# x Wx of 10 steps ahead of an LSTM's first step in place of 12, that of the other 54 spread over 22 steps in place of 21

## The chip, the cores and the metric

The kernel runs on one core of a Trainium2 chip. The metric is the device time of one execution in microseconds (us); the time before is the median of three runs, 312.17 us (311.90 to 312.34). The core's engines work side by side, each through its own queue of instructions in order: TensorE multiplies matrices (the profile calls it PE, and its weight loads PEld), VectorE (DVE) and ScalarE (ACT) work on elements, GpSimd is POOL, and SyncE (SP) issues most of the transfers.

## The reference

An LSTM over 64 steps (batch 32, 256 inputs, 256 hidden) is followed by three dense layers on all its outputs, whose weights are +1 or -1, and a residual:

```python
xW = jnp.einsum('ntd,dg->ntg', x, Wx) + b
def step(carry, xw_t):
    prev_h, prev_c = carry
    a = xw_t + prev_h @ Wh
    i, f, o = (jax.nn.sigmoid(a[:, s * Hd:(s + 1) * Hd]) for s in range(3))
    g = jnp.tanh(a[:, 3 * Hd:])
    next_c = f * prev_c + i * g
    next_h = o * jnp.tanh(next_c)
    return (next_h, next_c), next_h
h = jnp.concatenate([hs, -hs], axis=-1)
h = relu(s0 * (h @ sign(k0))) * 2      # 512 -> 1024
h = relu(s1 * (h @ sign(k1))) * 2      # 1024 -> 1024
out = x + s2 * (h @ sign(k2))          # 1024 -> 256
```

Here `sign` stands for +1 where the boolean weight is true and -1 elsewhere (the loop over the gates is written out in the original). The data are 32-bit floats.

## The kernel before

The 64 steps are a chain: step t needs h of step t - 1. Beside that chain TensorE has two kinds of work which are spread over the steps as cover: x Wx of later steps, then the dense layers (FFN) on blocks of 16 finished steps.

**Layout.** The 256 hidden units are cut into four quarters, the batch of 32 sits beside each, so that 4 x 32 = 128 partitions are full. The gate products (`gates_from_h`, L304 to L315) of one step are 16 matmuls, each with a 128x32 weight load (h transposed) and Wh streaming past: for each of the two PSUM banks (three gates of 64 columns in one, the output gate in the other), two halves of the contraction and four quarters. x Wx (`x_part`, L245 to L256) has the same form with 256 columns; four such matmuls for one half k of one step are two units of work, a step is four units, 8 matmuls, and two steps share a PSUM bank (`x_bank`), which `evict_x` adds the bias to and stores as tile `xg` (L265). When a unit is left over, the four matmuls are made in two halves of 128 columns, a unit each (L283 to L286).

**One step** (`cell_step`, L322 to L345): sigmoid of two gates, tanh, sigmoid of the output gate on ScalarE (L325 to L327), kept, new and c on VectorE (L329 to L333), tanh on ScalarE (L335), h and its transpose on VectorE (L337, L342), and then the copies of x Wx of the next step into the gate banks by ScalarE (L319, L320), onto which the next gate products add.

**FFN.** `ffn_block` (L588) works on 16 steps: h is split into two parts of reduced precision (`split_h`, L361 and L362), layer 0 (L594), layer 1 (L620) and layer 2 (L607) are matmuls with 128x128 weight loads and 512 columns, one unit each, 192 units a block. `evict` (L365 to L370) takes each result out of PSUM with ScalarE and VectorE (L368, L369). Three blocks lie in the loop, 576 units. The fourth, `last_block` (L433 on), comes after the last step, and uses sums of weight quarters (`make_sum`, L418) that VectorE makes during the loop. The output of a block is turned, scaled and stored a part per step (`output`, L373; L392, L395, L387).

**The order of the work** is written by hand; each engine's queue has the order of the program. Ahead of the first step stand the loads (x and Wx first, then Wh: two loads on SyncE's queue and two on ScalarE's, L142 to L144), products that warm TensorE up (L646), x Wx of the first 8 steps, then that of steps 8 up to `AHEAD` (L683), and the copy of step 0 into the gate banks (L685). The loop over t (L705) issues in each step the gate products, the cell, a part of an output if one is waiting (L711), and as many units of work as the goal asks for (L717 to L720). For t below `X_STEPS` the work is x Wx, with the whole number

```python
goal = (t + 1) * total_x // X_STEPS if t < X_STEPS else (t + 1 - X_STEPS) * total_ffn // (T - X_STEPS)
```

and from `X_STEPS` on it is the FFN. Before, that is 208 units on 21 steps (two steps of nine units, at t = 0 and t = 10, and 19 of ten) and 576 on 43 steps (13 or 14 each).

Behind these in each step come the smaller jobs: the transposes of later x on VectorE, each with a request for another half block of x on SyncE's queue (`next_x`, L267; L232, L96), splits of h, and "chores": conversions of the boolean weights (w0 on ScalarE and VectorE, L208 and L209; w1 and w2 on ScalarE, L214 and L218). `load[0]` counts the larger VectorE jobs of the step, and some of the smaller ones wait for a step in which it is below 2. Chores start at t = 2, those of w2 at t = 24, the sums at t = 28.

Of the kernel before, what the change touches and what calls it, by code (L numbers as in the profile page):

```python
# [43 lines left out]
def lstm_ffn(ctx: ExitStack, tc: tile.TileContext, x, cond, wx_d, wh_d, b_d, k0_d, k1_d, k2_d, s0_d, s1_d, s2_d, out):  # L44
# [14 lines left out]

    GATES = (3, 0, 1, 2)  # L60

    AHEAD = 12
    X_STEPS = 21

    FIRST_CHORE = 2
    W2_STEP = 24
# [200 lines left out]
    def next_x(half):  # L267

        if half < 2 * NB:
            load[0] += 1  # L270
            turn_x(*divmod(half, 2))
            if half + 4 < 2 * NB:
                load_x(*divmod(half + 4, 2), [nc.sync])

    def x_products(t0, t1):

        for t in range(t0, t1, 2):
            p = x_bank(t)
            for s in range(2):
                for k in range(2):  # L280
                    start = s == 0 and k == 0
                    passes = min(left_over[0], 2)
                    if passes == 1:  # L283
                        x_part(p, t + s, k, slice(0, 2), start)
                        yield 1
                        x_part(p, t + s, k, slice(2, 4), False)  # L286
                    else:
                        x_part(p, t + s, k, slice(0, 4), start)
                    if s == 1 and k == 1:
                        evict_x(p, t)  # L290
                        half, left = divmod(t + 2, SB // 2)
                        if left == 2 and half + 1 < 2 * NB:
                            turns.append(half + 1)
                        if left == 6 and turns:
                            next_x(turns.popleft())
                    yield passes
# [50 lines left out]
    def split_h(i):  # L347

        b, s = divmod(i, SB // SH)
        if s == 0:  # L350
            hparts[b] = (
                hpool.tile([P, 2, TB], F32R, tag="hhi", name=f"hhi{b}"),
                hpool.tile([P, 2, TB], F32R, tag="hlo", name=f"hlo{b}"),
            )
        hi, lo = (p[:, :, ts(s, SH * N)] for p in hparts[b])
        full = hist.pop(i)
        if b == NB - 1:

            hi, lo = (a.rearrange("p k (n t) -> p k t n", n=N) for a in (hi, lo))
            full = full.rearrange("p k (t n) -> p k t n", n=N)  # L360
        nc.scalar.copy(hi, full)  # L361
        nc.vector.tensor_tensor(lo, full, hi, ALU.subtract)  # L362
# [319 lines left out]
    nc.vector.transpose(hT, h_first.rearrange("p (j b) -> p b j", b=2))  # L682
    for _ in x_products(SB // 2, AHEAD):  # L683
        pass
# [3 lines left out]
    def ffn():  # L688
        for b in range(NB - 1):
            yield from ffn_block(b)  # L690
        yield from last_block(NB - 1)
# [8 lines left out]

    work = x_products(AHEAD, T)
    total_x = (T - AHEAD) * 4
    total_ffn = (NB - 1) * (4 * FC0 + 2 * FC0 * FC1 + 4 * FC1)
    done = 0
    for t in range(T):  # L705
# [5 lines left out]
        if outputs:  # L711
            load[0] += 1
            if next(outputs[0], "end") == "end":
                outputs.popleft()
        if t == X_STEPS:
            work, done = ffn(), 0
        goal = (t + 1) * total_x // X_STEPS if t < X_STEPS else (t + 1 - X_STEPS) * total_ffn // (T - X_STEPS)  # L717
        while done < goal:
            left_over[0] = goal - done
            done += next(work)  # L720
        if t == X_STEPS - 1:
            next(work, None)

        if turns and load[0] < 2:
            next_x(turns.popleft())
        if splits and (load[0] < 2 or t >= X_STEPS or t == SH * splits[0] + 2 * SH - 1):
            split_h(splits.popleft())
        else:
# [4 lines left out]
            elif t >= W2_STEP and chores2:  # L733
                chores2.popleft()()
            if w0_parts and (load[0] < 2 or t == X_STEPS - 1):
                w0_parts.popleft()()
# [34 lines left out]
```

## Time and profile before

| | before |
|---|---|
| median of three runs | 312.17 us (311.90 to 312.34) |
| the profiled execution's own time | 312.77 us |
| its span | 311.0 us |
| TensorE matmuls busy | 304.9 us (98%) |
| VectorE busy | 177.6 us (57%) |
| ScalarE busy | 143.1 us (46%) |
| TensorE's granted clock | 1.00 throughout |
| start of the first gate products on the chain | 17.64 us |
| start of the FFN work on the chain | 81.91 us |
| start of the last gate products on the chain | 260.08 us |

Busy times are shares of the span, and the starts are counted from the span's beginning. "The chain" is the work that ended last, followed back step by step to what released it; one line of it gives the start, the length, the engine, the tile and the line, and how many instructions are merged in it. A line of the waits gives who waited for whom, the time in total, how often, and the longest. "issue" means that the engine waited for nothing that the profile shows. A line of landings gives the time from a transfer's issue to its end.

### The profile page before, as it was taken

The numbers are of one execution on the slowest core, as the hardware profiler recorded it, in microseconds if no ns is written. First come the engines' busy times: TensorE is split into PE (matmuls) and PEld (weight loads), VectorE is DVE, ScalarE is ACT, GpSimd is POOL, SyncE is SP. The second block draws the span as 40 slices with busy tenths as digits, with TensorE's granted clock in tenths as the row PEclk, the third lists the DMA queues.
The fourth block names the chain that finished last, engine by engine and source line by source line (L and its number), as shares of the span: only waits on it lengthen the run. The fifth ranks groups of instructions, "written<-read, shape, count | busy, mean of one in ns | idle before, by whom it ended". The sixth has DMA issues, their size and how long they took to land.

```text
span 311.0 us, 9795 instructions
## 1 busy us (share of the span) xinstructions
PE 304.9 (98%) x4138; PEld 242.4 (78%) x4138; DVE 177.6 (57%) x527; ACT 143.1 (46%) x512; POOL 6.6 (2%) x24
## 2 busy tenths in 40 slices
PE   7999999999999999999999999999999999999994
PEld 3888888787777777777777777777777777899994
DVE  2466767777673444455755444568564444599441
ACT  0224657774564543444633433356443333786320
POOL 5300000000000000000000000000000000000000
PEclk9999999999999999999999999999999999999999
DMA  6864001143000000000010000000410000031001
GB/s 186 210 185 108 6 10 49 36 93 67 3 2 0 2 2 0 3 2 0 2 38 14 22 1 2 2 2 6 98 34 2 3 0 2 25 80 32 2 0 68
DMA packets 27450, 10.88 MB, mean 35 GB/s; under 512 B 23560, under 2 KB 26632, under 8 KB 27408
## 3 DMA queue, kind: packets, MB, share of 16 engines
q1 hardware_dynamic: 24768, 8.66, 11.3%
q10 hardware_dynamic: 2400, 1.57, 1.8%
q8 instruction: 32, 0.52, 0.7%
q14 instruction: 10, 0.08, 0.1%
q0 software_dynamic: 240, 0.04, 0.1%
HBM read 8.16 MB, written 2.10 MB: 33 GB/s over the span
## 4 chain that ended last, share of the span: by engine, by line
PE 96%; DMA 1%; DVE 1%; SPq 0%; ACT 0%; issue 0%; ACTq 0%
PE p L620 30%; PE gates L308 20%; PE px L249 18%; PE p L594 8%; PE po L607 7%; PE gates L459 4%; PE r L459 2%; PE x L459 2%; PE po L564 2%; PE p L486 2%; DMA wx<-in_L_cond_Wx_dram 1%; SPq L96 0%; DVE a_7l L369 0%; DVE o L574 0%; PE p_bias L661 0%
## 5 line engine op out<-in xcount | busy, mean ns | idle before, releaser
L308 PEld LDWEIGHTS gates<-wh,hist 128*32 128x32 f32 x2016 | 54.6, 109 | 22.3 <-issue 13.4
L308 PE MATMUL gates<-wh,hist 128*32 128x192 f32 x2016 | 68.1, 275 | 0.0
L249 PE MATMUL px<-wx,xT 128*32 128x256 f32 (+1 forms) x1168 | 60.7, 355 | 0.4 <-DMA wx<-in_L_cond_Wx_dram 0.4
L325 ACT ACTIVATE sig<-gates 128x128 f32<-128x128 f32 x64 | 17.7, 277 | 79.8 <-PE gates L308 79.6
L249 PEld LDWEIGHTS px<-wx,xT 128*32 128x32 f32 x1168 | 42.2, 111 | 12.3 <-DVE xT L232 1.3
L329 DVE TENSOR_TENSOR kept<-sig,c 128x64 f32<-128x64 f32 x63 | 14.2, 225 | 49.1 <-ACT sig L325 48.8
L335 ACT ACTIVATE th<-c 128x64 f32<-128x64 f32 x64 | 16.4, 257 | 31.4 <-DVE c L333 31.4
L337 DVE TENSOR_TENSOR h<-sig,th 128x64 f32<-128x64 f32 x64 | 14.4, 225 | 20.7 <-ACT th L335 20.7
L265 DVE TENSOR_TENSOR xg<-px,bias 128x512 f32<-128x512 f32 x32 | 21.2, 670 | 2.8 <-PE px L249 2.3
L319 ACT COPY gates<-xg 128x192 f32<-128x192 f32 x64 | 20.0, 313 | 1.5 <-DVE xg L265 1.5
L594 PE MATMUL p<-hhi,w 128*128 128x512 f32 x48 | 19.3, 402 | 0.0
L594 PE MATMUL p<-hlo,w 128*128 128x512 f32 x48 | 19.1, 397 | 0.0
L342 DVE STREAM_TRANSPOSE hist<-h 128x64 f32<-128x64 f32 x64 | 15.7, 245 | 2.4
L333 DVE TENSOR_TENSOR c<-kept,new 128x64 f32<-128x64 f32 x64 | 14.4, 225 | 2.2
L327 ACT ACTIVATE sig<-gates 128x64 f32<-128x64 f32 x64 | 14.9, 233 | 0.1
L326 ACT ACTIVATE cand<-gates 128x64 f32<-128x64 f32 x64 | 14.0, 218 | 0.0
L331 DVE TENSOR_TENSOR new<-sig,cand 128x64 f32<-128x64 f32 x64 | 13.9, 217 | 0.0
L320 ACT COPY gates<-xg 128x64 f32<-128x64 f32 x64 | 13.0, 203 | 0.0
L594 PEld LDWEIGHTS p<-hhi,w 128*128 128x128 f32 x48 | 9.0, 188 | 2.1
L594 PEld LDWEIGHTS p<-hlo,w 128*128 128x128 f32 x48 | 9.0, 188 | 1.9
L214 ACT ACTIVATE w<-bits,nsgn,sgn 128x1024 fp32r<-128x1024 uint8 x8 | 9.9, 1240 | 0.0
L620 PE MATMUL p<-a_7h,w 128*128 128x512 f32 x24 | 9.9, 412 | 0.0
(250 smaller groups left out, 603.1 us busy)
## 6 DMA issues: line engine op xcount, KB each, us to landing
x<-in_x_dram SPq DMA_DIRECT2D x52, 64.0 KB, 2.7
out_dram<-o SPq DMA_DIRECT2D x28, 64.0 KB, 1.8
bits<-in_L_ffn_k_dram SPq DMA_DIRECT2D x10, 128.0 KB, 2.7
wx<-in_L_cond_Wx_dram SPq DMA_DIRECT2D x2, 256.0 KB, 4.8
wx<-in_L_cond_Wx_dram ACTq DMA_DIRECT2D x4, 128.0 KB, 5.1
wh<-in_L_cond_Wh_dram ACTq DMA_DIRECT2D x2, 256.0 KB, 5.3
wh<-in_L_cond_Wh_dram SPq DMA_DIRECT2D x2, 256.0 KB, 5.8
k<-in_L_ffn_k_dram SPq DMA_DIRECT2D x2, 256.0 KB, 3.1
```

The lines of the kernel that those rows point to most:

```text
L249: nc.tensor.matmul(p[q * N : (q + 1) * N, t % 2, slots], xT[i // 2, i % 2][:, s, k, :], wx_q[:, k, q, slots], start=start, stop=False, ski ...
L265: nc.vector.tensor_tensor(xg[t], p.rearrange("p t g j -> p t (g j)"), b, ALU.add)
L308: nc.tensor.matmul(g[q * N : (q + 1) * N], hT[:, k, :], wh_q[:, k, q, slots], start=False, stop=(k == 1), skip_group_check=True,)
L319: nc.scalar.copy(gates[0], x_t[:, :3])
L325: nc.scalar.activation(sig[:, 0:2, :], gates[0][:, 1:3], AF.Sigmoid)
L327: nc.scalar.activation(sig[:, 2, :], gates[1][:, 0], AF.Sigmoid)
L335: nc.scalar.activation(th, c, AF.Tanh)
L342: nc.vector.transpose(hT, h.rearrange("p (j b) -> p b j", b=2))
L459: nc.tensor.matmul(bank[pair][:, i], a(k)[:, ts(2 * pair + i, P)], b(k, n), start=first and i == 0 and k == 0 and n == 0, stop=last and k ...
L594: nc.tensor.matmul(p, w0[:, k, ts(m, P)], a[:, k, :], start=(n == 0), stop=(n == 3))
L607: nc.tensor.matmul(po[m], w2[:, m, k], a1[k][n], start=(k == 0 and n == 0), stop=(k == FC1 - 1 and n == 1))
L620: nc.tensor.matmul(p1[m], w1[:, k, ts(m, P)], a0[k][n], start=(k == 0 and n == 0), stop=(k == FC0 - 1 and n == 1),)
```

## The change

Two constants. `AHEAD` says how many steps' x Wx is made ahead of the first step, `X_STEPS` over how many steps that of the rest is spread, and with it at which step the FFN begins.

```diff
     GATES = (3, 0, 1, 2)
 
-    AHEAD = 12
-    X_STEPS = 21
+    AHEAD = 10
+    X_STEPS = 22
```

What follows from the formula of the goal: x Wx of steps 10 and 11 moves from ahead of the loop into it; the loop's x Wx is (64 - 10) x 4 = 216 units on 22 steps, nine units at t = 0, 5, 11 and 16 and ten elsewhere; the FFN's 576 units lie on 42 steps, 30 of 14 units and 12 of 13. The smaller jobs come in partly other steps, since they follow the goal and `load[0]`: the four VectorE halves of the w0 conversions at t = 2, 10, 12 and 18 (before 6, 10, 14 and 18), the transposes of later x at t = 0, 3, 6, 9, 14 and 16 (before 0, 2, 5, 9, 13 and 15), the output of the first two blocks one step later, and the last sum of weight quarters at t = 60 (before 58). Each engine has the same instructions, in another order on TensorE, VectorE, ScalarE and SyncE.

## The prediction

> **What bounds the kernel now.** I read the page's busy shares first, then the chain of work that ended last (its shares, then its pieces in order of time), then the waits, and last the landings of the transfers that the first step needs.
>
> ```profile
> span 311.0 us, 9795 instructions
> PE 304.9 (98%) x4138; PEld 242.4 (78%) x4138; DVE 177.6 (57%) x527; ACT 143.1 (46%) x512; POOL 6.6 (2%) x24
> ...
> PE 96%; DMA 1%; DVE 1%; SPq 0%; ACT 0%; issue 0%; ACTq 0%
> ```
>
> TensorE is busy for 98% of the span and is 96% of the chain, so the time is a sum of TensorE work plus what little it waits. The chain in order of time (start, length, what) shows each step of the recurrence as a pair, its gate products (L308) and the cover behind them (L249 while x Wx lasts, L594, L620 and L607 afterwards):
>
> ```profile
> 10.74 6.91 PE px L249 x128
> 17.64 0.86 PE gates L308 x30
> 18.50 1.96 PE px L249 x40
> 20.46 0.92 PE gates L308 x32
> 21.38 2.16 PE px L249 x48
> 23.55 0.87 PE gates L308 x32
> ...
> 48.71 1.95 PE px L249 x40
> 50.66 0.93 PE gates L308 x32
> 51.59 2.16 PE px L249 x40
> ...
> 81.03 0.87 PE gates L308 x32
> 81.91 3.17 PE p L594 x13
> 85.08 1.01 PE gates L308 x32
> ...
> 103.03 3.40 PE p L620 x14
> 106.43 1.01 PE gates L308 x32
> ```
>
> The reader is to see three step lengths. With ten units of x Wx a step is 3.034 us (21.38 to 48.71 holds nine of them and 51.59 to 81.91 ten: 27.33 and 30.32 us). With nine units, at t = 0 and t = 10, it is 2.88 us (18.50 to 21.38, 48.71 to 51.59). In the FFN part a step of 13 units is 4.18 us (81.91 to 86.09) and one of 14 is 4.41 us (103.03 to 107.44); every FFN step from 81.91 to 260.08 has one of these two lengths, so nothing but TensorE's own work sets it.
>
> From the waits, one line (time in total, how often):
>
> ```profile
> PEld gates L308 <- issue: 13.4, 38, 0.4
> ```
>
> A weight load of the gates sat idle 0.35 us, with no releaser, in most of the 42 steps whose gates follow FFN work. Last, the answer for wh's two loads on ScalarE's queue (issued at 7.39 and 8.71 us), used below:
>
> ```profile
> DMA to landing us min/median/max: 3.8/5.3/6.7
> ```
>
> **The change, part by part.** The sum is made on this profiled execution, whose span is 311.0 us and whose own time is 312.77; the median of the three timed runs is 312.17, so the sum's difference is put on 312.17. A run differs from another by up to 0.44 us (311.90 to 312.34).
>
> 1. Ahead of the first step, x Wx of steps 10 and 11 goes: 2 steps x 8 matmuls = 16 matmuls of 128x256. The piece 10.74 to 17.64 holds 64 of them in 6.91 us (its x128 counts a load and a matmul each), 0.108 us apiece: -1.73 us. With them one addition of the bias (L265, 0.67 us) moves behind step 0; VectorE has room there, since it waits for TensorE in that stretch.
>
> 2. The x part of the loop has 54 x 4 = 216 units on 22 steps in place of 208 on 21. By the goal's whole numbers that is 18 steps of ten and 4 of nine (t = 0, 5, 11, 16), where before there were 19 and 2. 18 x 3.034 + 4 x 2.88 = 66.13 us against 19 x 3.034 + 2 x 2.88 = 63.41: +2.73 us. Split matmuls (two of 128 columns for one of 256) cost nothing: steps listed x48 and x40 both take 2.16. A nine-unit step should be one unit, 0.216, shorter than 3.034, that is 2.818; it measures 2.88, so its cover is too short by 0.06 us, and the chain sigmoid, cell, tanh, transpose shows through. Two more such steps are 0.13 of the 2.73.
>
> 3. The FFN part has 576 units on 42 steps in place of 43: 30 steps of 14 and 12 of 13, where before there were 17 and 26. 13 x 4.405 - 14 x 4.18 = -1.26 us. Why it is not zero: 14 units less 13 are 0.225 us, so a step has 4.18 - 13 x 0.225 = 1.25 us that are no FFN unit, while among x products the gates cost 0.87. The passage from FFN products (128x128 weights) to the gates (128x32 weights) and back costs 0.38 us a step: gates longer by 0.14, and 0.24 that the step's 13 units take beyond their pace. One passage of 43 goes.
>
> 4. What the earlier start uncovers. The first gate product (t = 0) would be issued 1.73 us earlier: its first matmul starts at 17.42 in the timeline, so at 15.69. It needs hT_first (transposed by 15.07), the copies of x Wx into its bank (by 12.84), and wh. The last wh load (slot 0, ScalarE's queue) was issued at 8.71 and landed 6.7 us later, at 15.41. A landing releases its reader some 0.16 to 0.22 us later (wx on SyncE's queue: 1.65 + 4.3 = 5.95, first product 6.11; x: 1.20 + 4.0 = 5.20, transpose 5.42). So wh is usable at 15.57 to 15.63: 0.06 us before it is wanted. Behind the waiting gate stand x products of TensorE's queue and all later steps, so any lateness is paid in full. Lower bound: nothing (no earlier start can gain more than 1.73). Upper bound: the four wh loads took 3.8, 5.0, 6.5 and 6.7 us, so a landing may be later by as much as the middle ones differ from the last, 6.7 - 5.3 = 1.4. I take +0.1, near the row of this very load.
>
> The Trainium skill (DMA: Bandwidth & Descriptors, Latency and other measured facts) speaks against the change here: it puts HBM access at 0.2 us on average and 2 us at high load, and this stretch moves some 180 GB/s. By the page alone, a load that met the high figure would be 1.8 us later (an estimate, 2 less 0.2) and take the whole earlier start back; this load's own row has it just in time.
>
> 5. Work that is only shifted against the steps. VectorE per x step keeps at most two large pieces behind the cell's own five: two of L265 (0.67), L232 (0.70), L209 (0.73) or one and L362 (0.47). In the three new short steps they are 22's addition with a split of h (t = 5), 36's with a split (t = 11), 48's with a transpose of x and a w1 conversion on ScalarE (t = 16). The two old short steps carried L265 with L232 (t = 0) and L265 with L209 and a w1 conversion of 1.24 us on ScalarE (t = 10): both fitted, kept (L329) starting 0.30 us after sig as everywhere. So the new ones are costed at nothing; without that cover each piece of 0.70 us too many would be paid once. In FFN steps VectorE's heaviest load (t = 51: a transposition, three L369, one L362) is the same as before, and TensorE there is ahead of a chain of 1.9 us by cover of 3.17 or more. SyncE's queue issues the same 43 rows; x of steps 48 to 63 is requested at t = 0 and t = 3 in place of t = 0 and t = 2, wanted many steps later. The four transfers for x of steps 16 to 23 land by about 16.4 us and are wanted near 19, where they were wanted at 20.9. POOL's queue is untouched. The output of blocks 0 and 1 starts one step later (t = 37 in place of 36, t = 51 in place of 50), and the last sum of weight quarters goes from t = 58 to t = 60; its product comes at about 290 us. The last recurrence step has 14 units in both, so the tail, with its 0.54 us wait for a_7l, stays.
>
> Sum: -1.73 + 2.73 - 1.26 + 0.1 = -0.16 us. On 312.17 that is 312.0.
>
> **The rivals.** A difference under 0.2%, 0.62 us, can't be told from no change.
> - The likeliest: as summed, 312.0, within 0.2%.
> - No passage is saved: what item 3 counts for one is paid again elsewhere in the FFN steps. For: the 0.35 us idle has no releaser. Against: steps of 13 and of 14 differ by a pure unit. Then -1.73 + 2.73 - 0.87 (the moved gates at the cheap price in both places) + 0.1 = +0.2: 312.4, also within 0.2%.
> - Slower, wh late: the first gates wait for the last piece of wh. For: 0.06 us of room. Against: the room is not negative in this execution, and earlier loads in the same queue set the first x product too, so a late queue moves both. Each us beyond 15.6 costs a us; it decides from a wait of 0.9 (-0.26 + 0.9 = +0.64). With a wait of 1.2: 313.1.
> - Slower, short steps don't fit: VectorE's pieces delay kept in the three new places by half of an 0.7 us piece each: -0.16 + 3 x 0.35 = +0.9, 313.1. Against: the old short steps carried as much.
> - Faster, the waits at the end of the recurrence go too: shifted evictions free a_7l earlier, and 0.54 us fall away: -0.16 - 0.54 = -0.7, 311.5. Against: the last step's units and their order are unchanged.
>
> **How the numbers follow.** Chances: the sum 0.62, no saved passage 0.12, wh late 0.09, short steps 0.07, the tail 0.10. Same is the first two, 0.74; slower 0.09 + 0.07 = 0.16; faster 0.10. The predicted time is the likeliest case's, 312.0. With the runs' own 0.44 us of spread the first two cases reach from 311.6 to 312.6; the range goes to 311.4, which takes in the tail's case, and to 312.9, which leaves out the larger part of the two slow ones.
>
> **What would show it.** Right: the piece of x products ahead of the first gates is 5.18 us long, and the first gates start near 15.9 on the chain; 22 steps of x products, four of them 2.88 us long; FFN steps only of 4.18 and 4.41, thirty of the longer; start of the FFN part at 82.9 (81.91 - 1.73 + 2.73) and the last gates near 259.8 before any wait for wh. Wrong: a gap on TensorE ahead of the first gates released by the wh transfer (wh late); short steps above 2.95 (they don't fit); FFN steps of other lengths (no saved passage); no wait for a_7l near 263 (the tail). The prediction fails if any one stall of over 0.6 us appears that the trace of before hides, and the first gates are where the room is least.

## The result, and the profile after

The changed kernel takes 313.83 us (median of 6 runs, 313.64 to 315.76) against 312.12 us for the kernel before in the same comparison: a ratio of 1.0059, with a 95% interval from 1.0044 to 1.0073. It is slower by 1.7 us, where a difference inside 0.6 us was forecast. The profiled execution took 313.79 us, with a span of 312.0. The two profiled executions differ by only 1.0 us, since the one of before took 312.77, 0.6 above its median. By the starts on their chains the difference of the spans is -1.93 up to the first gates, +2.72 from there to the FFN's start, +0.48 from there to the last gates and -0.27 behind them.

```profile
span 312.0 us, 9797 instructions
PE 305.7 (98%) x4138; PEld 241.9 (78%) x4138; DVE 178.5 (57%) x527; ACT 143.4 (46%) x512; POOL 6.6 (2%) x24
...
PE 94%; DVE 2%; DMA 1%; ACT 1%; issue 0%; SPq 0%; ACTq 0%
```

The page's busy shares (its first part) hardly move. The shares of the chain of work that ended last (its fourth part) do: TensorE goes from 96% to 94%, ScalarE and VectorE together from 1% to 3%. Where they come in is seen in the chain in order of time (start, length, what), read at the start of the steps, at the end of x Wx and around the end of a block of the FFN:

```profile
10.53 5.18 PE px L249 x96
15.71 0.86 PE gates L308 x30
16.57 1.96 PE px L249 x40
18.53 0.92 PE gates L308 x32
19.45 2.16 PE px L249 x48
...
82.70 3.17 PE p L594 x13
85.87 1.01 PE gates L308 x32
86.88 3.40 PE p L594 x14
90.27 1.01 PE gates L308 x32
...
134.67 3.40 PE p L620 x14
138.07 0.83 PE gates L308 x16
138.98 0.29 ACT sig L325
139.29 0.23 DVE kept L329
139.52 0.15 DVE new L331
139.69 0.23 DVE c L333
139.94 0.26 ACT th L335
140.20 0.22 ACT gates L319
140.56 0.54 ACT a_7h L368
141.12 0.70 DVE a_7l L369
141.87 1.43 PE po L607 x5
143.29 1.01 PE gates L308 x32
```

The first lines answer to those shown of before: 5.18 us of x products in place of 6.91, short steps of 2.88 us (16.57 to 19.45), FFN steps of 4.18 (82.70 to 86.88) and 4.40. The lines from 138.98 to 141.87, on ScalarE and VectorE and then the products that waited for them, are new at this place. The step that begins with the gates at 138.07 (t = 35) lasts 5.22 us until the next gates, where one of 14 units lasts 4.41. The same stands at 199.68 (t = 49), with 5.24 us; before, such a wait stood only at t = 63. The waits name it (who waited for whom, in total, times, longest):

```profile
PEld po L607 <- DVE a_7l L369: 1.6, 3, 0.5
PEld po L607 <- ACT a_7h L368: 0.9, 2, 0.4
```

Before there was one such wait, the 0.54 us at t = 63:

```profile
PEld po L607 <- DVE a_7l L369: 0.5, 1, 0.5
```

It is the loop's last step, and it loses some 0.4 us (4.83 us from its gates to the last block's first products, where 14 units take 4.41).

The timeline of the changed kernel around 140 us (start, length, engine, line, and in brackets the idle time ahead and what ended it) shows how it comes about. a_7h and a_7l are the two parts that layer 1's last tile is split into when it is taken out of PSUM:

```profile
139.34 0.40 PE L620 MATMUL p<-a_7l,w 128*128 128x512 f32 x1
...
140.36 0.20 ACT L320 COPY gates<-xg 128x64 f32<-128x64 f32 x1
...
140.50 0.59 ACT L368 ACTIVATE a_7h<-p 128x512 fp32r<-128x512 f32 x1
...
140.72 0.39 PE L607 MATMUL po<-a_5l,w 128*128 128x512 f32 x1
...
141.12 0.69 DVE L369 SCALAR_TENSOR_TENSOR a_7l<-p,a_7h 128x512 fp32r<-128x512 f32 x1 [0.38 <-ACT a_7h L368]
...
141.14 0.49 PE L607 MATMUL po<-a_7h,w 128*128 128x512 f32 x1
```

Layer 1's last tile is complete when the matmul of 139.34 ends, at 139.74. Its eviction by ScalarE (a_7h, L368) starts at 140.50, right behind the cell's copies into the gate banks (L319, L320), because the program puts it behind them in ScalarE's queue. TensorE has six layer 2 products that don't need this tile, the last of them at 140.72, and then waits for a_7h and again for a_7l.

Why at every block now: 576 units on 42 steps are 13.714 a step, and a block of 192 units is exactly 14 steps. So each of the three blocks ends with a step; its last step begins 14 units before the block's end. The last 12 of these are layer 2 products, which the program puts behind layer 1's last tile, so that tile is completed by the step's second unit, early in the step, while ScalarE is still bound to the cell. With 43 steps a block was 14.33 steps, and only the third ended with one (the last step had 14 units in both kernels).

The sum over the FFN steps: from the FFN's start to the last gates the changed kernel takes 261.35 - 82.70 = 178.65 us against 260.08 - 81.91 = 178.17. The prediction had 1.26 less, 176.91. The difference of 1.74 us is (5.22 - 4.405) + (5.24 - 4.405) = 1.65 (4.405 us is the usual step of 14 units), and a rest of 0.09, of which some hundredths stand at the steps behind these two (4.19 and 4.23 us in place of 4.18). With the 1.65 the prediction's sum of -0.16 us becomes +1.5; measured are +1.7, and +1.5 lies inside the interval.

### The profile page after: what moved, and what is told of

Same layout as the page of the kernel before. It is cut to its first block, busy times and chain, and to the rows that moved or that the text cites. A ratio compares the mean times of both kernels' runs of the same rounds, so it can differ in the third digit from the quotient of the medians.

```text
span 312.0 us, 9797 instructions
## 1 busy us (share of the span) xinstructions
PE 305.7 (98%) x4138; PEld 241.9 (78%) x4138; DVE 178.5 (57%) x527; ACT 143.4 (46%) x512; POOL 6.6 (2%) x24
## 4 chain that ended last, share of the span: by engine, by line
PE 94%; DVE 2%; DMA 1%; ACT 1%; issue 0%; SPq 0%; ACTq 0%
PE p L620 29%; PE gates L308 20%; PE px L249 18%; PE p L594 8%; PE po L607 6%; PE gates L459 4%; PE r L459 2%; PE x L459 2%; PE po L564 2%; PE p L486 2%; DMA wx<-in_L_cond_Wx_dram 1%; DVE a_7l L369 1%; ACT a_7h L368 0%; ACT sig L325 0%; SPq L96 0%
## 5 line engine op out<-in xcount | busy, mean ns | idle before, releaser
L319 ACT COPY gates<-xg 128x192 f32<-128x192 f32 x64 | 20.0, 313 | 1.3 <-DVE xg L265 1.3
L320 ACT COPY gates<-xg 128x64 f32<-128x64 f32 x64 | 13.0, 203 | 0.0
L620 PE MATMUL p<-a_0h,w 128*128 128x512 f32 x24 | 9.7, 404 | 0.0
```

The costliest lines, as they stand in the source:

```text
L319: nc.scalar.copy(gates[0], x_t[:, :3])
L620: nc.tensor.matmul(p1[m], w1[:, k, ts(m, P)], a0[k][n], start=(k == 0 and n == 0), stop=(k == FC0 - 1 and n == 1),)
```

## The experiments

All were compared with runs of the kernel before on the same chip (medians of 312.19 to 312.27 us). Each variant has a name, by which later texts and the table speak of it.

**Two units earlier (e1_plus2).** The goals of the FFN are two units higher in the changed kernel.

```diff
-(t + 1 - X_STEPS) * total_ffn // (T - X_STEPS)
+min(total_ffn, (t + 1 - X_STEPS) * total_ffn // (T - X_STEPS) + 2)
```

> The changed kernel, with every FFN goal two units higher (the last step has 12 units in place of 14), so that the last two products of layer 1's last tile of a block fall into the step before the one that ends the block. Theory A (in the changed kernel 576 units on 42 steps make a block exactly 14 steps; layer 1's last tile is finished as the second unit of the block's last step, its eviction stands on ScalarE behind that step's cell, and layer 2 has only 6 units to cover it; two new waits of 0.8 us and the old one at t = 63): the waits for a_7h and a_7l are gone, 2 x 0.82 and some 0.4 at t = 63 come back: 313.83 - 2.0 = 311.8, or by the prediction's sum 312.12 - 0.26 - 0.4 = 311.5. Theory B (the cost lies in the earlier first step or in the 22 steps of x Wx): 313.8, since these are not touched.

Measured: 312.39 us, a ratio to before of 1.0004 (95% interval 0.9995 to 1.0013, as in the brackets of the later results). The loss is gone but for 0.2 us, and no wait for a_7h or a_7l by layer 2 is left. The chain at the same end of a block:

```profile
135.24 3.40 PE p L620 x14
138.63 1.01 PE gates L308 x32
139.64 2.94 PE po L607 x12
142.59 0.45 PE p L594 x2
143.04 1.01 PE gates L308 x32
```

The step is 4.41 us again. The cause in the FFN is shown: nothing about the x part was touched. But 312.39 is 0.6 above the expected 311.8, and 0.9 above what the prediction's sum would give, so something else costs. One part stands in the trace: the first 32 products of the last block (L486) take 7.48 us here and 7.26 in the changed kernel, since they wait for the last split of h (`hlo`, L362), which now comes after a shorter last step. This 0.22 us is in all three executions with the goals two units higher (42.01 us from the first of these products to the start of VectorE's last instruction) and in none of the others (41.78 to 41.80).

**The same alignment made in the kernel before (e2_aligned).**

```diff
         goal = (t + 1) * total_x // X_STEPS if t < X_STEPS else (t + 1 - X_STEPS) * total_ffn // (T - X_STEPS)
+        goal = {33: 178, 34: 192, 47: 370, 48: 384}.get(t, goal)
```

> The kernel before, with four of its 43 FFN goals moved: t = 33 at 178 units, 34 at 192, 47 at 370, 48 at 384, so that blocks 0 and 1 end with a step and layer 1's last tile is finished as that step's second unit; 12 and 21 stay. Theory A: two waits of 0.8 us appear: 312.12 + 1.6 = 313.8. Theory B: 312.1, as before.

Measured: 314.84 us, 1.0078 (1.0064 to 1.0092), 2.6 us slower than before. The two waits appear, in the same total as in the changed kernel (1.6 and 0.9 us with the third at t = 63), and the two steps take 5.24 and 5.22 us. The expectation was too low, because the edit does more: it puts four units in the step after the second block, which takes 2.82 us where 1.25 + 4 x 0.225 = 2.15 would do if the cell's chain were covered, another 0.67. 0.83 + 0.81 + 0.67 = 2.3 of the 2.6 us.

**Each constant alone.** X_STEPS at 22 with 12 steps ahead (e3_12_22), and 10 steps ahead with X_STEPS at 21 (e4_10_21):

```diff
-    X_STEPS = 21
+    X_STEPS = 22
```

> X_STEPS 22 alone, 12 steps ahead: 208 units on 22 steps, 10 of ten and 12 of nine, 42 FFN steps. Theory A: x part 10 x 3.034 + 12 x 2.88 - 63.41 = +1.49, FFN steps -1.26, two waits +1.64: 312.12 + 1.9 = 314.0. Theory B (earlier first step): no earlier start here, +1.49 - 1.26 = +0.2: 312.3.

Measured: 314.05 us, 1.0055 (1.0043 to 1.0068): 1.8 us slower, with steps of 5.22 us at t = 35 and t = 49. The alignment comes with X_STEPS alone.

```diff
-    AHEAD = 12
+    AHEAD = 10
```

> AHEAD 10 alone, 21 steps: 216 units, 15 steps of ten and 6 of eleven (3.25 us), FFN on 43 steps as before. Theory A: -1.73 + (15 x 3.034 + 6 x 3.25 - 63.41 = +1.60) = -0.13: 312.0. Theory B: the loss of the earlier start shows here too, 313.5 or more.

Measured: 312.86 us, 1.0017 (1.0008 to 1.0027). No wait at the ends of the first two blocks, but 0.6 us slower than before where the sum had 0.1 faster. So there is a cost beside the alignment. The profiled executions place a part of it ahead of the first gates (times in us by the timeline; x Wx's end is that of its last matmul ahead of the gates; e5_plus1 and e6_order are the changed kernel with edits to the FFN alone, described below):

| | steps ahead | start of x Wx | its end | first gates | gates less end |
|---|---|---|---|---|---|
| before | 12 | 6.11 | 17.65 | 17.42 | -0.23 |
| e2_aligned | 12 | 5.85 | 17.09 | 16.85 | -0.24 |
| e3_12_22 | 12 | 6.15 | 17.33 | 17.09 | -0.24 |
| changed | 10 | 6.05 | 15.71 | 15.48 | -0.23 |
| e4_10_21 | 10 | 5.61 | 15.45 | 15.49 | +0.04 |
| e1_plus2 | 10 | 5.73 | 15.23 | 15.51 | +0.28 |
| e5_plus1 | 10 | 5.62 | 15.33 | 15.61 | +0.28 |
| e6_order | 10 | 5.70 | 15.77 | 15.54 | -0.23 |

With 12 steps ahead the gates follow x Wx at once (matmuls overlap by 0.23 us). With 10 ahead the gates never start before 15.48 in these five executions, however early x Wx is done: counted from the usual overlap, they are late by 0.27 us in e4_10_21 and by 0.51 in e1_plus2 and e5_plus1, and not at all in the changed kernel and e6_order, where x Wx itself ended late enough. In e1_plus2's timeline:

```profile
9.81 5.42 PE L249 MATMUL px<-wx,xT 128*32 128x256 f32 x96
...
15.48 0.95 PEld L308 LDWEIGHTS gates<-wh,hT_first 128*32 128x32 f32 x32 [0.73 <-issue]
15.51 1.08 PE L308 MATMUL gates<-wh,hT_first 128*32 128x192 f32 x32 [0.28 <-issue]
```

These are the start, the length and, in brackets, the idle time ahead; the profile gives no releaser ("issue"). The other inputs of the first gates were there: `hT_first` at 14.38 and the copies into the gate banks at 12.14. The candidate is wh's slot 0, issued last on ScalarE's queue, at 8.7 us, and landing 6.6 us later, at 15.3. In e5_plus1, whose gates start latest, it landed latest of the five, at 15.4.

This wait is not what made e4_10_21's profiled execution slow. Its FFN starts at 81.57 us (before 81.91), and its last gates at 259.75 (before 260.08). From the start of VectorE's last instruction to the end of the span it takes 4.94 us, where the eleven executions with other constants take 4.03 to 4.31: the last four stores landed 2.9 to 3.1 us after their issue, in those 2.2 at most. Why is open.

**One unit earlier (e5_plus1).** The size of the wait, in place of its presence:

```diff
-(t + 1 - X_STEPS) * total_ffn // (T - X_STEPS)
+min(total_ffn, (t + 1 - X_STEPS) * total_ffn // (T - X_STEPS) + 1)
```

> The changed kernel with every FFN goal one unit higher. Theory A: layer 1's last tile is now finished as the first unit of a block's last step, its eviction still stands behind that step's cell on ScalarE, and one product less lies between the start of the step and the wait for it: each of the three waits grows by one unit, 0.227 us, 0.7 us in all: 313.83 + 0.7 = 314.5. If the waits only depend on a block ending with a step: two units moved removed them, one should about halve them, 313.1 or so.

Measured: 314.51 us, 1.0074 (1.0061 to 1.0087), 0.7 us slower than the changed kernel; the steps at t = 35 and t = 49 take 5.46 and 5.45 us, one unit more than 5.22 and 5.24. So moving one unit makes it worse and moving two makes it vanish: what counts is whether the eviction of layer 1's last tile stands ahead of the last step's cell in ScalarE's queue or behind it.

**Two products more as cover (e6_order).**

```diff
-        yield from layer2([(0, last - 2), (0, last - 1), (1, last - 2)])
-        yield from layer2([(0, last), (1, last - 1), (1, last)])
+        yield from layer2([(0, last - 2), (0, last - 1), (1, last - 2), (1, last - 1)])
+        yield from layer2([(0, last), (1, last)])
```

> The changed kernel, goals as they are, but layer 2's last products in the order (0,5) (0,6) (1,5) (1,6) (0,7) (1,7), so that 8 products in place of 6 stand ahead of the first one that needs layer 1's last tile. Theory A: the three waits shrink by up to 0.45 us each: 0.82 to 0.36 twice, 0.4 to 0 at t = 63, -1.3 in all: 312.5. If the wait has nothing to do with the eviction's lateness: 313.8.

Measured: 312.58 us, 1.0015 (1.0005 to 1.0025), 1.25 us faster than the changed kernel; the steps are 4.76 and 4.78 us, 0.46 less each, and two waits are left in place of three:

```profile
PEld po L607 <- DVE a_7l L369: 1.0, 2, 0.5
```

Both sizes came as worked out from a late eviction and a cover of so many products.

**Wh's last load earlier.** In e1_plus2 (the new variant is e9_wh_pool), and in the kernel before as the control (e10_before_wh_pool):

```diff
-    load_gates(wh, wh_d, (0,), [nc.scalar])
...
         scales.append(s)
+    load_gates(wh, wh_d, (0,), [nc.gpsimd])
```

> e1_plus2 with wh's slot 0, the load that landed last (15.3 us in e1_plus2, 15.4 in before, 15.3 in e4_10_21), issued on GpSimd's queue, behind the small loads there, so that it starts some 3 us earlier. Theory C (with 10 steps ahead the first gates stand at 15.5 us, released by this load, whenever x Wx is done earlier): the first gates start at the end of x Wx, near 15.0, 0.3 to 0.5 us faster than e1_plus2: 312.0. Without such a wait: 312.4, or slower if GpSimd's load takes bandwidth from Wx.

> The same move of wh's slot 0 in the kernel before, as the control. Theory C: with 12 steps ahead the first gates come at 16.9 us or later, long after the load, so it stays at 312.2. If it becomes faster here too, by 0.3 or more, the move gains in another way (the start of x Wx), and e9_wh_pool says nothing on the wait.

Measured: 311.87 us (0.9988, 0.9979 to 0.9997), 0.5 faster than e1_plus2 (measured on another chip; its ratio to before was 1.0004), while the control stays, 312.27 us (1.0004, 0.9996 to 1.0013). The gates follow x Wx at once again: in e9_wh_pool its matmuls end at 15.85 and the gates start at 15.61. But in that execution TensorE waited instead for Wx (0.51 us in the middle of its first products, which the expectation had as a risk), so its trace shows the wait gone and not the gain; the gain of 0.5 us stands only in the medians.

The same move with 10 steps ahead and 21 steps (e11_10_21_wh_pool):

> e4_10_21 (10 steps ahead, 21 steps, FFN as before; 312.86, where the prediction's sum without a wait gives 312.0) with wh's slot 0 on GpSimd's queue. Theory C: the wait for wh at the first gates is what is left over, so some 0.5 us come back as from e1_plus2 to e9_wh_pool: 312.3. If the move only helped e1_plus2 by chance, 312.9.

Measured: 312.62 us, 1.0011 (0.9993 to 1.0029). Between the two expectations, 0.24 us below e4_10_21, and the interval holds both no gain and all of it: inconclusive. Its first gates follow x Wx at once (which ends at 15.63, and they start at 15.39), but the end of the span is late here too: 4.66 us from the start of VectorE's last instruction, and the last four stores landed 2.8 to 3.0 us after their issue. So the last wh load is not shown to be the whole of the 0.6 us: in e4_10_21's own execution the late stores (0.6 us or more) weigh more than the wait for wh (0.27).

**Putting it together.** The order of layer 2 alone in the kernel before (e8_before_order), and all three edits on the changed constants (e12_all):

> The kernel before with the order of e6_order alone: there one of the three waits exists, at t = 63. Theory A: that 0.4 us goes, and nothing else: 312.2 - 0.4 = 311.8. Otherwise 312.2.

> e9_wh_pool (10 and 22, goals two units higher, slot 0 of wh on GpSimd's queue; 311.87) with the order of e6_order as well. Theory A: the waits are gone already, so nothing more comes of the order: 311.9. If some wait for layer 1's last tile was left, less.

Measured: 312.03 us, 0.999 (0.9981 to 0.9999), for the order alone in the kernel before, 0.24 us where 0.4 was expected; its one wait for a_7l is gone, and in its profiled execution the last step takes 4.43 us in place of 4.83. And 311.78 us, 0.9985 (0.9976 to 0.9993), for 10 and 22 with the goals two units higher, the order and the earlier load, which agrees with e9_wh_pool's 311.87: the order brings nothing once the wait is gone. It is the fastest version of the study, 0.5 us ahead of the kernel before. Its first gates start at 15.25, earlier than in any execution with 10 steps ahead whose wh came by ScalarE's queue.

## Why the prediction was wrong

What was right: item 1 and the pieces of item 2: 5.18 us of x Wx ahead, 22 steps with four of 2.88 us (at t = 0, 5, 11 and 16); from the chain's first gates to the FFN's start 66.99 us, against the 64.27 of before and the forecast's 2.73 more, 67.00. Item 3's price of a step: the others are 4.18 and 4.41 as before, so the FFN part without its two waits would have come out within 0.1 us of the forecast. Item 5's costs of the x part, nothing, held too.

The step that failed is in item 5: "TensorE there is ahead of a chain of 1.9 us by cover of 3.17 or more", together with "so the tail, with its 0.54 us wait for a_7l, stays". The rows of before do show that no FFN step waits, but this rests on the alignment that they had. The one wait at t = 63 was read as a matter of the tail; it is a matter of a block that ends with a step, and 576 / 42 x 14 = 192 could have been worked out from the goal's formula. Two new waits of 0.82 us were costed at nothing. The cover that item 5 named, 3.17 us of TensorE work per step, covers the gates' chain, not the eviction behind it, which only has the 6 products that don't need the tile. The prediction did say that it fails if a stall of over 0.6 us appears that the trace of before hides, but it looked for it at the first gates.

The term of item 4 was in the right place, but one number could not size it. The wait for wh was put at +0.1 from one execution; in the five with 10 steps ahead and this load on ScalarE's queue it is nothing twice (in the changed kernel's own among them), 0.27 once and 0.51 twice. Its upper bound was also misread: 5.3 is the middle of the two loads on ScalarE's queue (3.8 and 6.7), not the landing time of a load. What remains open is the rest of e4_10_21's 0.6 us: its sum is -0.13 without a wait and +0.14 with the 0.27 of its profiled execution, and the late stores at its end have no cause on record.

Of the rivals, the slow one "wh late" named a real cost, of up to half a microsecond in the traces and not the 0.9 that it needed to decide. "Short steps don't fit" and "no passage is saved" did not happen; "faster" looked at the very wait that decides and expected it to vanish, where it came back twice.

The Trainium skill (PSUM — Partial Sum Buffer, Engine vs sequencer instructions) says of ScalarE's queue that it is strict first in, first out. The rows agree: a_7h's tile was complete at 139.74 and its eviction started at 140.50, right behind the copies ahead of it (the last of them runs from 140.36 for 0.20 us). From the figures of the other page (DMA: Bandwidth & Descriptors, Latency and other measured facts) the prediction worked out an estimate of a load that is 1.8 us later. No run here shows that: in the nine executions with this load on ScalarE's queue it landed 6.1 to 7.2 us after its issue, 6.7 in that of before, and the waits of up to half a microsecond came with x Wx being earlier.

## What to carry to other kernels

When work with an inner period (here a block of 192 units) is spread over steps with a fixed count each, work out where the period's ends fall within a step, before and after: the cover at such an end is only the products that don't need the last result, and a wait that shows once in the profile of before may be that end, and not the tail. In an engine with an ordered queue, an eviction that becomes ready just after a step's chain has entered the queue is late by what is left of that chain (0.76 us here). Finishing the tile in the step before (here by moving two products; moving one made it worse) took the wait away, at 0.22 us in the last block, and putting two more products ahead of the tile's first reader took 0.46 us off each step. A start that is moved forward should be compared with the landing of each transfer that it needs over several executions, since one execution's room of 0.06 us was another's wait of 0.5.

## What the runs showed of the hardware that was not expected

The start of x Wx, which waits for transfers, varies by half a microsecond between executions (5.61 to 6.15 us in those of the table), and the time from the end of VectorE's last instruction to the end of the span, the last stores, from 3.55 us in e3_12_22 (308.95 to 312.5) to 4.46 in e4_10_21 (306.84 to 311.3). Both are as large as the effects that were sized here, so a profiled execution is best read by its stretches, and a total from the medians.
